# A graph network on one core: reordered transfers, masks kept from layer to layer, and products of exact bf16 parts

## The chip, the core and the metric

The kernel runs on one core of a Trainium2 chip. The metric is device time in microseconds, lower is better; the kernel before is a median of three runs. The engines are called here as the profile calls them: PE (TensorE, with PEld for its weight loads), DVE (VectorE), ACT (ScalarE), POOL (GpSimd) and SP (SyncE, which only issues transfers here). [...]

## What is computed

Two graph-attention layers and a two-layer perceptron, on 6,250 nodes of 768 features and 100,000 edges sorted by destination:

```python
h = jnp.maximum(_layernorm(x, axis=-1), 0.0)
# gat_conv, with 4 heads in layer 1 and 1 head in layer 2; every node also has an edge to itself
h = (x @ W).reshape(n, heads, -1)
alpha_s = (h * a_src[None]).sum(-1)
alpha_d = (h * a_dst[None]).sum(-1)
e = jax.nn.leaky_relu(alpha_s[src] + alpha_d[dst], NEG_SLOPE)
...
alpha = e / (denom[dst] + 1e-16)
out = jax.ops.segment_sum(h[src] * alpha[:, :, None], dst, num_segments=n)
# after both layers, each followed by relu
h = jax.nn.relu(h @ Wm1 + bm1)
return h @ Wm2 + bm2        # and x + this is the result
```

The hidden width is 256 and everything is float32.

## The kernel before

The nodes are cut into 49 tiles of 128 (the last has 106). The edges, padded, make 784 tiles of 128, in 196 groups of four; a group's destinations lie in a moving window of nodes that steps by 32.

**Stage 1** (the loop over `i` with `moments`, `spread_means`, `centre`, `features1`, `keep1`, from line 252) normalizes x and multiplies it by W1. For a tile, x comes twice, as rows (`xt`, for the statistics) and transposed (`xTt`, for the product), each 384 KB. DVE computes mean and variance; PE spreads the means over the free dimension by a product with the identity (L218); DVE subtracts (L224), ACT takes relu, PE makes six products of 128x264 (L233), and ACT and POOL put the row together that goes to `table1` in HBM (L244). The loop runs three tiles ahead with its moments and fetches five tiles ahead. W1 has eight more columns, W1 times the attention vectors, which PE computes from the transposed weights (`scores_in`, L147). The edge indices are loaded on ACT's queue, and `edge_places` turns them, piece by piece between the tiles, into places inside the window: `dcol` as columns, `dmod_d` as bf16 rows in HBM.

**Edge layers** (`layer_edges`, run for layer 1 and then for layer 2). POOL gathers the source rows of each edge tile from the table (L339), ten groups ahead, one indirect transfer for every tile. `fetch_rows` (L349) broadcasts 16 tiles of `dmod_d` to all partitions, and `make_mask` (L362) compares them with the partition number: a bf16 0/1 mask of eight tiles, that is, of two groups. PE multiplies the masks with the destinations' factors (L383). `pair` computes the weights of two tiles (ACT L401, L403, DVE L406 and following), and PE adds up the rows by destination in `o_ps` (L429). `gather_up` folds a group's sum into the running sum (L442); finished strips of 32 nodes are copied to `sum` (L455), and with the last strip of a node tile its steps are appended to `late`, to be run one at a time between the pairs by `advance`.

**Node work.** In layer 1, `Node1` adds the node's own edge, divides, transposes, multiplies by W2 and writes `table2` (L552). In layer 2, `Node2` does the same and then the perceptron; `prefetch` loads the node's row and x, `ahead` adds the bias bm2, broadcast to all partitions, to x (L617), and the last steps add that to the product in `y_ps` (L646, L650) and store the result (L651).

The order on each engine is the program's order inside the blocks under `tc.manual_schedule()`, of which there are three, one for each stage; between them a scheduler places what stands outside. [...]A tile of a pool comes free when its last reader is done.

Of the kernel before, what the change touches and what calls it, by code (L numbers as in the profile page):

```python
# [47 lines left out]
def kernel(  # L48
# [39 lines left out]
    make_identity(nc, ident)  # L88
    iota = const.tile([P, P], F32, name="iota")
# [53 lines left out]
    def scores_in(ps, w, wt, a, K, H):  # L143
        p = ps.tile([P, K, 2 * H], F32, name="aps", tag="e")
        for k in range(K):
            for j in range(KH):
                nc.tensor.matmul(p[:, k], wt[:, j, k * P:(k + 1) * P], a[:, j],  # L147
                                 start=(j == 0), stop=(j == KH - 1))
        nc.vector.tensor_copy(w[:, :, HID:], p)

    def load_x(xp, i):
        n = min(P, N - i * P)
        t = xp.tile([P, IN_DIM], F32, name="xt", tag="xt")
        if n < P:
            nc.vector.memset(t, 0.0)
        nc.sync.dma_start(t[:n], x[i * P:i * P + n])
        return t, n
# [4 lines left out]
    def edge_places(ones):  # L162

        dst_i = ones.tile([P, NET], I32, name="dst_i")
        nc.scalar.dma_start(dst_i, dst_cols)
        dri = ones.tile([NCH, CH], I32, name="dri")
        nc.scalar.dma_start(dri, dst_rows)
        nc.scalar.dma_start(src_i, src_cols)
        for layer in bT:
            with nc.allow_non_contiguous_dma(reason="256 numbers"):  # L170
                nc.scalar.dma_start(bT[layer], {1: b1, 2: b2}[layer].rearrange("(k p) -> p k", p=P))
        yield
# [15 lines left out]
        nc.scalar.dma_start(dmod_d, drm)  # L188
# [3 lines left out]
    bT = {layer: const.tile([P, KH], F32, name=f"bT{layer}") for layer in (1, 2)}  # L192
    with tc.tile_pool(name="w1p", bufs=1) as wp, tc.tile_pool(name="x1", bufs=6) as xp, \
            tc.tile_pool(name="wk1", bufs=3) as wk, tc.tile_pool(name="once", bufs=1) as ones, \
            tc.manual_schedule():
        xs, xTs, means, cents, rs = {}, {}, {}, {}, {}

        def fetch(i):
            xs[i], _ = load_x(xp, i)
            xTs[i] = xp.tile([P, KI, P], F32, name="xTt")  # L200
            nc.sync.dma_start(xTs[i], xT[i].rearrange("p (k n) -> p k n", k=KI))

        def moments(i):
# [9 lines left out]
            means[i] = mv, std, rstd  # L213

        def spread_means(i):
            mv, _, rstd = means[i]
            m_ps = ps.tile([P, P], F32, name="mean_ps", tag="n")
            nc.tensor.matmul(m_ps, mv[:, 0:1].to_broadcast([P, P]), ident, start=True, stop=True)  # L218
            means[i] = m_ps, rstd
# [26 lines left out]
        fetch(0)  # L246
        loaded = weights_in(wp, W1T, A1, KI, 4, "w1")
        fetch(1)
        w1 = wp.tile([P, KI, HID + 8], F32, name="w1")
        nc.sync.dma_start(w1[:, :, :HID], W1.rearrange("(k p) f -> p k f", p=P))  # L250
        for i in range(2, 5):
            fetch(i)
        pieces = edge_places(ones)
        next(pieces)
        for i in range(-3, NT):
            if i == 0:
                scores_in(ps, w1, *loaded, KI, 4)
            if 0 <= i:
                if i + 5 < NT:
                    fetch(i + 5)  # L260
                h = features1(i)
            if i + 3 < NT:
                moments(i + 3)
            if 0 <= i + 2 < NT:
                _, std, rstd = means[i + 2]
                nc.vector.reciprocal(rstd, std)
                spread_means(i + 2)
            if 0 <= i + 1 < NT:
                centre(i + 1)
            if 0 <= i:  # L270
                keep1(i, *h)
                if i >= 2:
                    next(pieces, None)
# [42 lines left out]

    def layer_edges(layer, H, node, pre, matched):
# [3 lines left out]
        with tc.tile_pool(name=f"g{layer}", bufs=AHEAD + 2) as gp, \  # L321
                tc.tile_pool(name=f"rows{layer}", bufs=3) as rows, \
                tc.tile_pool(name=f"eg{layer}", bufs=2) as eg, \
# [3 lines left out]
            G, drow, mask, hot, e_ps, o_ps = {}, {}, {}, {}, {}, {}  # L327
# [5 lines left out]
            def gather(g):  # L333
                if not 0 <= g < NG:
                    return
                G[g] = gp.tile([P, TPG, TW[layer]], F32, name="G")
# [5 lines left out]

            def fetch_rows(r):

                k = 16 * r
                if 0 <= k < NET:
                    drow[r] = rows.tile([P, 16 * P], BF16, name="drow")
                    n = min(16, NET - k) * P
                    nc.sync.dma_start(drow[r][:, :n], bcast(dmod_d, n, k * P))  # L349
# [5 lines left out]
            def make_mask(u):  # L355

                if not 0 <= u < NU:
                    return
                a, b = (t * P for t in both(u))
                mask[u] = eg.tile([P, 8 * P], BF16, name="mask")  # L360
                at = u % 2 * 8 * P
                nc.vector.tensor_scalar(mask[u][:, a:b], drow[u // 2][:, at + a:at + b], pidx, None,  # L362
                                        ALU.is_equal)

# [69 lines left out]
            def gather_up(g):  # L434
# [3 lines left out]
                acc = sums.tile([P, RW[layer]], F32, name="acc")  # L438
                if g == 0:
                    nc.vector.tensor_copy(acc, o_ps.pop(g))  # L440
                else:
                    nc.vector.scalar_tensor_tensor(acc, run[0], keep[:, (g + 1) % 4:(g + 1) % 4 + 1],  # L442
                                                   o_ps.pop(g), ALU.mult, ALU.add)
                run[0] = acc
                a = g - 2
                if a < 0:
                    return
                t, q = divmod(a, 4)
                if q == 0:
                    done[t] = sums.tile([P, RW[layer]], F32, name="sum", bufs=3)  # L450
                    node.prefetch(t)
                if q == 2:
                    node.ahead(t)
                r = slice(32 * q, 32 * q + 32)
                nc.scalar.activation(done[t][r], acc[r], AF.Copy)  # L455
                if g == NG - 1:
                    node.ahead(t)
                    nc.vector.tensor_copy(done[t][64:], acc[64:])
                    q = 3
                if q == 3:  # L460
                    late.append(node.steps(t, done.pop(t)))
# [7 lines left out]
            for r in range(3):  # L469
                fetch_rows(r)  # L470
            for u in range(2):
                make_mask(u)
# [6 lines left out]
            for g in range(NG):  # L479
# [7 lines left out]
                else:  # L487
                    if g % 4 == 0:
                        fetch_rows(g // 4 + 3)
# [6 lines left out]
                hot.pop(g, None)  # L496
            gather_up(NG - 1)
# [18 lines left out]
    with tc.tile_pool(name="w2p", bufs=1) as wp, tc.tile_pool(name="wk2", bufs=2) as wk:  # L516
        w2 = with_scores(ps, wp, W2, W2T, A2, KH, 1, "w2")

        class Node1:
# [12 lines left out]
            def steps(self, t, sum_):  # L532
# [13 lines left out]
                for k in range(KH):  # L546
                    nc.tensor.matmul(h_ps, rT[:, k], w2[:, k], start=(k == 0), stop=(k == KH - 1))
# [7 lines left out]
        with tc.tile_pool(name="pre1", bufs=1) as pre:  # L555
            pre1 = prepare(pre, 1, 4)
            with tc.manual_schedule():
                layer_edges(1, 4, Node1(), pre1, lambda: None)


    with tc.tile_pool(name="wmp", bufs=1) as wp, tc.tile_pool(name="x3", bufs=3) as xp, \
            tc.tile_pool(name="wk3", bufs=2) as wk, tc.tile_pool(name="pre2", bufs=1) as pre, \
            tc.manual_schedule():
# [3 lines left out]
        bm2b = wp.tile([P, OUT_DIM], F32, name="bm2b")  # L567
# [4 lines left out]
        def matched():  # L572
# [6 lines left out]
            nc.scalar.dma_start(bm2b, bcast(bm2, OUT_DIM))  # L579
# [20 lines left out]
        class Node2:  # L600
            rows, xs = {}, {}

            def prefetch(self, t):
# [4 lines left out]
                nc.sync.dma_start(self.xs[t][0][:n], x[t * P:t * P + n])  # L608
# [6 lines left out]
            def ahead(self, t):  # L615
                xt, n = self.xs[t]
                nc.vector.tensor_add(xt[:n], xt[:n], bm2b[:n])  # L617

            def steps(self, t, sum_):
# [23 lines left out]
                for s in range(2):  # L643
                    y_ps[s] = ps.tile([P, half], F32, name="y_ps", tag="n")
                    for j in range(KH):
                        nc.tensor.matmul(y_ps[s], mT[:, j], wm2[:, j, s * half:(s + 1) * half],  # L646
                                         start=(j == 0), stop=(j == KH - 1))
# [3 lines left out]
                nc.sync.dma_start(out[t * P:t * P + n], y[:n].rearrange("p s f -> p (s f)"))  # L651
# [301 lines left out]
```

## Time and profile before

| | |
|---|---|
| timed runs | 2784.78 us (2783.95 to 2788.01) |
| the profiled execution | 2218.71 us, span 2216.9 us |
| mean granted PE clock | 0.808 |
| gathers, L339 | 1564, 962 ns each |
| HBM read and written | 335.80 MB and 32.50 MB |

The profiled execution was a quarter shorter than the timed ones. All rows of the profile below belong to the shorter one.

The page cuts the span into 40 slices of 55 us. Stage 1 fills the first three and a part of the fourth, layer 1 goes from 187 to 1180 us, layer 2 from there to the end. In the tables a group of instructions has its busy time, the mean of one in ns, and then the idle time of its engine ahead of it with what ended most of it. "Issue" means that the engine waited for nothing that the profile shows. In the rows of the timeline the columns are start, duration, engine, line, operation, output and inputs with their shapes, count, and in brackets the idle time before and its releaser. In the rows of windows they are the window, its length, and for PE, PEld, DVE, ACT and POOL the busy time with the number of instructions, then PE's granted clock, the busy share of the DMA engines and GB/s.

### The profile page before, as it was taken

Reading aid. Unit: us, or ns where it says so; the run is one execution under the profiler, and the core shown is the slowest. Engines: PE = TensorE matmul, PEld = TensorE weight load, DVE = VectorE, ACT = ScalarE, POOL = GpSimd, SP = SyncE. Lnnn points to the kernel's source line nnn. Section 1 sums busy time; section 2 is a strip of 40 time slices with the busy share of each in tenths; the row PEclk is TensorE's granted clock in tenths of the full one; section 3 lists DMA queues with packets and bytes.
Section 4 is the critical chain, followed back from the end, with each engine's and each line's share of the span. In section 5 each row is a group of like instructions: output and inputs, shape, how many; then the busy total and the mean of one; then the engine's idle time right before and its main releaser. Section 6 shows DMA issues by size and latency. Waiting matters only on the chain. (4 is left out here: it accounts for less than half of the span.)

```text
span 2216.9 us, 25764 instructions
## 1 busy us (share of the span) xinstructions
PE 1581.7 (71%) x6588; PEld 1099.4 (50%) x6589; DVE 1480.5 (67%) x4510; ACT 599.4 (27%) x2602; POOL 1518.4 (68%) x1672
## 2 busy tenths in 40 slices
PE   7995766676667676666675777677877777777776
PEld 6783444444444444444443455555555554555553
DVE  6665677777777677777775666666666666666663
ACT  3552222222222222222222222222222222222221
POOL 0004777777777777777775777777777777777773
PEclk9997777877887877887886798888777878778786
DMA  8893555555555555545545565565556556555652
GB/s 288 291 306 109 143 145 151 151 139 148 152 152 141 146 151 151 150 139 150 151 122 172 162 182 158 183 182 165 177 181 182 166 174 183 171 166 182 181 143 89
DMA packets 149839, 370.16 MB, mean 167 GB/s; under 512 B 34354, under 2 KB 60978, under 8 KB 149684
## 3 DMA queue, kind: packets, MB, share of 16 engines
q0 software_dynamic: 75072, 209.10, 35.0%
q1 hardware_dynamic: 72052, 156.47, 21.3%
q10 hardware_dynamic: 2560, 2.86, 0.4%
q8 instruction: 56, 0.92, 0.2%
q14 instruction: 99, 0.81, 0.1%
HBM read 335.80 MB, written 32.50 MB: 166 GB/s over the span
## 5 line engine op out<-in xcount | busy, mean ns | idle before, releaser
L339 POOL DMA_INDIRECT G<-table,src_i x1564 | 1504.4, 962 | 496.1 <-issue 404.8
L429 PE MATMUL o_ps<-hw,hot 128*128 128x260 f32 x1564 | 590.8, 514 | 319.0 <-DVE hw L418 310.9
L429 PE MATMUL o_ps<-G,hw 128*128 128x258 f32 x1564 | 564.2, 497 | 260.2 <-DVE hw L413 255.9
L429 PEld LDWEIGHTS o_ps<-hw,hot 128*128 128x128 f32 x1564 | 345.1, 244 | 503.8 <-DVE hw L418 436.2
L429 PEld LDWEIGHTS o_ps<-G,hw 128*128 128x128 f32 x1564 | 339.2, 238 | 425.5 <-DVE hw L413 371.7
L406 DVE TENSOR_TENSOR e_ps<-e,e_ps 128x8 f32<-128x8 f32 (+1 forms) x782 | 129.6, 166 | 550.9 <-ACT e L403 550.8
L455 ACT ACTIVATE sum<-acc 32x260 f32<-32x260 f32 (+1 forms) x388 | 161.7, 417 | 696.7 <-DVE acc L442 695.5
L413 DVE TENSOR_SCALAR hw<-iota_ps,dcol,w 128x128 f32<-128x128 f32 x782 | 285.0, 406 | 14.4
L401 ACT ACTIVATE e<-G 128x8 f32<-128x8 f32 (+1 forms) x782 | 158.9, 203 | 471.1 <-DMA G<-table,src_i 452.1
L418 DVE TENSOR_TENSOR hw<-G,e_ps 128x520 f32<-128x520 f32 x391 | 271.8, 695 | 14.5 <-DVE e_ps L416 1.2
L442 DVE SCALAR_TENSOR_TENSOR acc<-acc,keep,o_ps 128x260 f32<-128x260 f32 (+1 forms) x390 | 185.7, 476 | 3.3 <-PE o_ps L429 3.3
L233 PE MATMUL h_ps<-w,r 128*128 128x264 f32 x588 | 146.5, 401 | 13.2 <-ACT r L226 13.1
L403 ACT ACTIVATE e<-G 128x8 f32<-128x8 f32 (+1 forms) x782 | 150.0, 192 | 0.2
L646 PE MATMUL y_ps<-wm,mT 128*128 128x384 f32 x392 | 143.1, 488 | 1.3 <-ACT mT L640 0.9
L372 DVE TENSOR_TENSOR hot<-iota_ps,dcol 128x512 f32<-128x512 f32 (+1 forms) x196 | 133.8, 682 | 0.0
L233 PEld LDWEIGHTS h_ps<-w,r 128*128 128x128 f32 x588 | 112.2, 197 | 33.5 <-ACT r L226 15.5
L243 POOL COPY row<-sd 128x4 f32<-128x4 f32 x49 | 9.1, 186 | 170.0 <-ACT sd L242 170.0
L512 ACT ACTIVATE rT<-tp,bT 128x128 f32<-128x128 f32 x196 | 61.2, 363 | 159.6 <-PE tp L505 159.3
L362 DVE TENSOR_SCALAR mask<-drow,pidx 128x1024 bf16<-128x1024 bf16 (+1 forms) x196 | 96.4, 493 | 2.2 <-DMA drow<-dmod_d 2.2
L383 PEld LDWEIGHTS <-mask 128*128 128x128 bf16 x1564 | 73.3, 101 | 42.6 <-issue 18.4
L646 PEld LDWEIGHTS y_ps<-wm,mT 128*128 128x128 f32 x392 | 74.2, 190 | 34.1 <-ACT mT L640 1.4
L207 DVE BATCH_NORM_STATS2 stats<-xt 128x6 f32<-128x384 f32 x98 | 49.9, 551 | 51.0 <-DMA xt<-in_x 50.4
(385 smaller groups left out, 1091.4 us busy)
## 6 DMA issues: line engine op xcount, KB each, us to landing
drow<-dmod_d SPq DMA_DIRECT2D x98, 512.0 KB, 5.6
xt<-in_x SPq DMA_DIRECT2D x96, 384.0 KB, 4.2
G<-table,src_i POOLq DMA_INDIRECT x1564, 2.8
xTt<-in_xT SPq DMA_DIRECT2D x49, 384.0 KB, 4.7
out<-y SPq DMA_DIRECT2D x48, 384.0 KB, 3.3
table<-row SPq DMA_DIRECT2D x49, 132.0 KB, 3.5
row<-table SPq DMA_DIRECT2D x49, 130.0 KB, 5.6
table<-row SPq DMA_DIRECT2D x49, 129.0 KB, 2.8
```

What stands on the lines that cost most here:

```text
L233: nc.tensor.matmul(h_ps, r[:, k], w1[:, k], start=(k == 0), stop=(k == KI - 1))
L339: nc.gpsimd.indirect_dma_start(out=G[g][:, t], out_offset=None, in_=table[layer], in_offset=bass.IndirectOffsetOnAxis(ap=src_i[:, k:k + 1] ...
L372: nc.vector.tensor_tensor(hot[g][:, T[0]:T[0] + n], iota_ps.unsqueeze(1).to_broadcast([P, n, P]), dcol[:, k:k + n].unsqueeze(2).to_broadca ...
L401: nc.scalar.activation(e1, sc, AF.Exp)
L403: nc.scalar.activation(e2, sc, AF.Exp, scale=SLOPE)
L406: nc.vector.tensor_mul(v, e2, rho)
L413: nc.vector.tensor_scalar(hw[:, t], iota_ps, dcol[:, k:k + 1], w[:, t], ALU.is_equal, ALU.mult)
L418: nc.vector.tensor_mul(hw, G[g][:, T, :RW[1]].rearrange("p t (h c) -> p t h c", h=H), w.unsqueeze(3).to_broadcast([P, 2, H, C + 1]))
L429: nc.tensor.matmul(o_ps[g], l, r[:, :RW[layer]], start=(k == tiles(g)[0]), stop=(k == TPG - 1))
L442: nc.vector.scalar_tensor_tensor(acc, run[0], keep[:, (g + 1) % 4:(g + 1) % 4 + 1], o_ps.pop(g), ALU.mult, ALU.add)
L455: nc.scalar.activation(done[t][r], acc[r], AF.Copy)
L646: nc.tensor.matmul(y_ps[s], mT[:, j], wm2[:, j, s * half:(s + 1) * half], start=(j == 0), stop=(j == KH - 1))
```

## The change

It has six parts:

- **Order of the first transfers.** Only tile 0's x goes ahead of W1's transposed weights; then come tile 0's transposed x, W1, and tile 1. The scores' product is done before tile 1 is looked at. The edge indices move from ACT's queue to SP's, between the tiles.
- **Loads and stores of 106 rows** are split in 96 and 10 rows (`runs`); the last store also in two column halves.
- **Means as bf16 products.** From tile 2 on, POOL splits the mean in three bf16 parts whose sum is exact (`in_parts`), and PE makes three bf16 products in place of one float32 product.
- **Layer 2's masks from layer 1.** Layer 1 stores each mask in HBM (`mask_d`, 256 KB for two groups), and layer 2 loads it instead of fetching the rows and comparing again.
- **The last bias on PE.** bm2 is split in three bf16 parts; a product of ones (3x128) with them (3x384) starts each accumulation of `y_ps`, and the addition to x in `ahead` is gone.
- **Smaller ones.** One manual schedule spans all stages; the pools of gathered rows, rows and masks are shared by both layers; the last group's sum is used where it lies; `prefetch` and `ahead` are called some groups earlier; W2's scores are computed inside layer 1's start.

```diff
+        eng.tensor_copy(parts[0], f)
+        eng.tensor_sub(a, f, parts[0])
+        eng.tensor_copy(parts[1], a)
+        eng.tensor_sub(b, a, parts[1])
+        eng.tensor_copy(parts[2], b)
...
+        return [(a, b) for a, b in ((0, n // 16 * 16), (n // 16 * 16, n)) if a < b]
...
-        nc.sync.dma_start(t[:n], x[i * P:i * P + n])
+        for a, b in runs(n):
+            nc.sync.dma_start(t[a:b], x[i * P + a:i * P + b])
...
-        nc.scalar.dma_start(dst_i, dst_cols)
-        nc.scalar.dma_start(dri, dst_rows)
-        nc.scalar.dma_start(src_i, src_cols)
+        for to, of in ((dst_i, dst_cols), (dri, dst_rows), (src_i, src_cols)):
+            nc.sync.dma_start(to, of)
+            yield
+            yield
...
-            nc.tensor.matmul(m_ps, mv[:, 0:1].to_broadcast([P, P]), ident, start=True, stop=True)
+                for k in range(3):
+                    nc.tensor.matmul(m_ps, parts[:, k:k + 1].to_broadcast([P, P]), ident_b,
+                                     start=(k == 0), stop=(k == 2))
...
-        fetch(0)
+        fetch_x(0)
         loaded = weights_in(wp, W1T, A1, KI, 4, "w1")
-        fetch(1)
+        fetch_xT(0)
         w1 = wp.tile([P, KI, HID + 8], F32, name="w1")
         nc.sync.dma_start(w1[:, :, :HID], W1.rearrange("(k p) f -> p k f", p=P))
-        for i in range(2, 5):
-            fetch(i)
+        for i in range(1, 5):
+            fetch_x(i)
+            fetch_xT(i)
         pieces = edge_places(ones)
-        next(pieces)
-        for i in range(-3, NT):
-            if i == 0:
-                scores_in(ps, w1, *loaded, KI, 4)
+        moments(0)
+        spread_means(0)
+        sc1 = scores(ps, *loaded, KI, 4)
+        centre(0)
+        nc.vector.tensor_copy(w1[:, :, HID:], sc1)
+        for i in range(-2, NT):
...
+                if layer == 2:
+                    return fetch_mask(u + 1)
...
                 nc.vector.tensor_scalar(mask[u][:, a:b], drow[u // 2][:, at + a:at + b], pidx, None,
                                         ALU.is_equal)
+                nc.sync.dma_start(mask_d[u * P:(u + 1) * P], mask[u])
...
+                if last:
+
+                    late.append(node.steps(t, acc))
...
                     if g % 4 == 0:
-                        fetch_rows(g // 4 + 3)
+                        if layer == 1:
+                            fetch_rows(g // 4 + 3)
+                        node.prefetch(g // 4)
+                    else:
+                        node.ahead(g // 4)
...
+                if layer == 1 and g == NG - 3:
+                    for k in range(3):
+                        fetch_mask(k)
...
-                nc.vector.tensor_add(xt[:n], xt[:n], bm2b[:n])
+                pass
...
+                    nc.tensor.matmul(y_ps[s], ones_r, bm2r[:, s * half:(s + 1) * half],
+                                     start=True, stop=False)
                     for j in range(KH):
                         nc.tensor.matmul(y_ps[s], mT[:, j], wm2[:, j, s * half:(s + 1) * half],
-                                         start=(j == 0), stop=(j == KH - 1))
+                                         start=False, stop=(j == KH - 1))
                     yield 1
                 for s in range(2):
                     nc.vector.tensor_add(y[:n, s], y_ps[s][:n], xt[:n, s * half:(s + 1) * half])
-                nc.sync.dma_start(out[t * P:t * P + n], y[:n].rearrange("p s f -> p (s f)"))
+                    if t == NT - 1:
+                        for a, b in runs(n):
+                            nc.sync.dma_start(out[t * P + a:t * P + b, s * half:(s + 1) * half],
+                                              y[a:b, s])
+                if t < NT - 1:
+                    nc.sync.dma_start(out[t * P:t * P + n], y[:n].rearrange("p s f -> p (s f)"))
```

## The prediction

> **What bounds the kernel now.** I read the page's busy totals and slices first, then windows over the two edge layers, then the gathers' starts in the timeline, and last the timeline at the four places where GpSimd is idle.
>
> ```profile
> PE 1581.7 (71%) x6588; PEld 1099.4 (50%) x6589; DVE 1480.5 (67%) x4510; ACT 599.4 (27%) x2602; POOL 1518.4 (68%) x1672
> ...
> PEclk9997777877887877887886798888777878778786
> DMA  8893555555555555545545565565556556555652
> ...
> L339 POOL DMA_INDIRECT G<-table,src_i x1564 | 1504.4, 962 | 496.1 <-issue 404.8
> 187.00:1170.00 983.00, 659.19 (x2626) 432.02 (x2625) 709.30 (x1998) 239.46 (x1162) 743.92 (x782) 0.79 0.53 145
> 1186.00:2185.00 999.00, 739.71 (x3168) 517.57 (x3168) 640.47 (x2186) 262.20 (x1204) 760.48 (x782) 0.80 0.58 173
> ```
>
> The totals name no bound: four engines are at 67 to 71%. The windows do. 782 gathers lie in each layer, and no other engine is above 74% busy there. GpSimd's gap before a gather is nearly always "issue": it waits for no one. In the timeline a gather starts 1.25 us after the last one (0.95 busy, 0.30 issue) almost without exception. So the layers last as long as their gathers: 187.83 to 1168.70 is 781 steps of 1.256 us, 1186.64 to 2184.07 is 781 of 1.277. Against 1.25 they lose 4.6 and 21.2 us. The time to win is in four places: before the first gather (188 us), between the layers (17 us), after the last gather (33 us), and those 21 us.
>
> ```profile
> 1507.63 0.95 DVE L617 TENSOR_TENSOR xt<-xt,bm2b 128x768 f32<-128x768 f32 x1
> 1508.31 1.10 POOL L339 DMA_INDIRECT G<-table,src_i  x1 [0.30 <-issue]
> 1509.56 0.48 DVE L362 TENSOR_SCALAR mask<-drow,pidx 128x1024 bf16<-128x1024 bf16 x1
> 1509.71 1.15 POOL L339 DMA_INDIRECT G<-table,src_i  x1 [0.30 <-issue]
> 1511.16 0.95 POOL L339 DMA_INDIRECT G<-table,src_i  x1 [0.30 <-issue]
> ```
>
> In layer 2 the slow gathers stand beside two VectorE operations, the bias addition (L617) and the mask (L362). Summed over the layer, gathers beside L617 lose 9.4 us, those beside L362 10.1 us.
>
> ```profile
> 13.86 5.24 PEld L147 LDWEIGHTS aps<-w1a,w1T 128*128 128x128 f32 x24
> 19.60 5.02 PE L233 MATMUL h_ps<-w,r 128*128 128x264 f32 x12 [0.40 <-ACT r L226]
> 169.61 1.02 DVE L207 BATCH_NORM_STATS2 stats<-xt 128x6 f32<-128x384 f32 x2 [6.99 <-DMA xt<-in_x]
> 172.74 5.25 PE L233 MATMUL h_ps<-w,r 128*128 128x264 f32 x12 [5.66 <-ACT r L226]
> 1168.70 0.94 POOL L339 DMA_INDIRECT G<-table,src_i  x1 [0.30 <-issue]
> 1186.64 0.94 POOL L339 DMA_INDIRECT G<-table,src_i  x1 [17.00 <-DMA drow<-dmod_d]
> 2184.07 0.95 POOL L339 DMA_INDIRECT G<-table,src_i  x1 [0.30 <-issue]
> 2205.49 0.56 DVE L650 TENSOR_TENSOR y<-y_ps,xt 106x384 f32<-106x384 f32 x1 [0.73 <-PE y_ps L646]
> ```
>
> The first features wait until 19.6 us behind the scores' matmuls, themselves queued behind tile 1's mean. The last tile's x (106 rows), issued at 159.3, is there at 169.6; a 128-row load lands in a median of 4.2 us. The last y is written at 2206.05 and the span ends at 2216.9: the 106-row store takes 10.8 us, a full one 3.3.
>
> [...] Four o_ps records take 1.14 or 2.10 us here.
>
> **Part by part**, in us of the profile.
>
> *Start.* Only tile 0's x now stands before the scores' transposed weights, and W1 comes third, before x of tile 1; 1.2 MB of indices leave the first 20 us. Scores' weights land near 6; [...] W1 (2.4 MB at the 290 GB/s of the page's first slices[...]) lands near 11. TensorE then takes tile 1's mean, which needs x of tile 1 (3.1 MB: 13.2, an estimate). Features start near 13.7 instead of 19.6: **-6**.
>
> *Node means.* Two fp32 records (0.36 of the tile's pitch, the rest being 2.53 of weight loads) become three bf16 products with their own weight loads. The mask products, 8 in 0.47 at most, give 0.06 each: 0.18. The tile pitch is 2.89 now, so 2.71; 47 tiles give -8.5 if TensorE limits. But 0.92 MB a tile in 2.71 us is 340 GB/s, and the best 20 us window moves 327 with the DMA engines 94% busy. I take 2.8 us, **-4**, with 0 and -8.5 as ends. The five GpSimd operations a tile (about 1 us, from 0.19 for its copy of a few columns) wait for the tile's moments; behind them on GpSimd stands only the table row of three tiles before, which nobody reads in this stage. GpSimd has 1.4 us of work in 20, and the products are used a tile later: hidden.
>
> *Stalls in stage 1.* 49 tiles at 2.89 should end near 163; they end at 183.6. Of the 20, about 8 belong to the last tile's x, now split in 96 and 10 rows; about 5 lie at 60 to 76 us, where the 1.5 MB of `drow` was fetched early and VectorE stood on it; that fetch now follows the last table row. The rest is x coming late and may stay. **-10**, ends -8 and -13. The start as a whole: **-20** (ends -14, -27).
>
> *Layer 1.* 98 mask writes of 256 KB: 25.7 MB. At 145 GB/s for a 0.53 share they add 94 us of DMA time to 983: the share goes to 0.63. A gather has 40 tiles of lead, so **0**. On SyncE each store waits for VectorE's mask, and behind it stand the next `drow`, the node rows and layer 2's table rows: each has a group (5 us) or more to spare, and the mask precedes them on VectorE anyway. The `w2` scores now run after two mask stores in SyncE's queue, so the first pairs start some 5 us later; VectorE (72%) and TensorE catch up within the 50 us of lead: **0**.
>
> *Between the layers.* The last table row was issued at 1180.77, between fetches of 512 KB, and the first gather came 5.9 us later; a row store lands in 2.8. The masks now come from an earlier fetch: -3. The last sum is used without copying: -0.8. **-4**.
>
> *Layer 2.* L617 is gone, 98 masks are gone: **-19** of the 21.2. Instead 98 bias products of 3x384 bf16 run on TensorE. The trace has none of this width: at least 0.06, at most the 0.36 of an fp32 record of 384 columns; I take 0.2, 20 us on an engine 74% busy, hidden. The earlier prefetch of x waits on SyncE for the buffer of three tiles before, two groups after its release: 0.
>
> *Tail.* The last store in halves of 96 and 10 rows lands in about 3.3 plus one issue (0.4) instead of 10.8: -6.5. The 106-row load no longer stands in the gathers' way (ScalarE stood 3.8 us for one at 2184): -2.4. Sum used directly -0.8, bias products +0.3. **-9.5**.
>
> The split of bm2 into parts in stage 1 (five small VectorE operations, two transfers of kilobytes) lies under that stage's DMA and TensorE time: 0.
>
> Sum: -20 -4 -19 -9.5 = **-52 us** of 2217.
>
> **From profile to time.** The profiled execution took 2218.7, the timed ones 2784.8, 568 more, and the trace cannot say where. If everything is slower alike, -52 becomes -65; if it is a constant, or 0.36 us on each gather, it stays -52. I take the middle, -57: **2728**.
>
> **Rivals.** (a) *DMA keeps stage 1 where it is.* VectorE's 50 us of waits for x speak for it, the share of 0.9 too. Then the start gives -10: -42, times 1.13: 2737; with half of layer 2's losses staying as well, 2750. (b) *In the timed runs TensorE is slow and bounds the layers.* A slow clock would explain part of the 568, but with all records at half rate a group of layer 1 takes 5.0 us (two times 2.10, masks 0.2, a quarter of 0.63 and 1.93 for the node), one of layer 2 6.1 (0.63, 2.07 and 4.3), a tile of stage 1 6.0: 196 groups of each, 49 tiles and 60 us of gaps make about 2540 only. Then masks and the bias addition give nothing, the bias products cost up to 35, means -20, start -6, middle -3, tail -9: -3, 2782. (c) *The mask traffic slows the gathers*, which would be so if the unprofiled gathers are limited by DMA. A median landing of 2.8 us speaks against it. At most 94 us less 52: +42, 2827, slower.
>
> **Chances.** Forecast 0.67, (a) 0.16, (b) 0.08, (c) 0.09. The forecast's own ends are -45 x 1.0 and -70 x 1.26: 2740 and 2697. The range, 2696 to 2780, leaves out (c), most of (b) and a little beyond the low end. Faster 0.83, same 0.07, slower 0.10.
>
> **What would show it.** First gather near 168; a 1.255 us step in layer 2 and no 1.15 us gathers beside masks; 13 us between the layers; 23 us after the last gather; DMA share in layer 1 near 0.63 with gathers still landing in 2.8. A longer step in layer 1, or "DMA" as the releaser of GpSimd, would make it wrong; so would time that does not follow the span.

## The result: 0.8% slower, and a profile with another bound

The changed kernel takes 2805.36 us (2802.69 to 2808.06) where the kernel before, run beside it, takes 2784.36 (2777.70 to 2788.01): a ratio of 1.0078, 95% interval 1.0057 to 1.0100. The forecast was 2728. This time the profiled execution, 2805.3 us, is as long as the timed ones, so its rows show what the times are made of; the profile of the kernel before (2218.7 us) was of an execution a quarter shorter, and that difference turns out to be the subject of this study. Which chip that first profile came from is not known.

The page of the kernel after, engine totals, the gathers and the relu of the transposed node tile:

```profile
PE 1711.7 (61%) x6733; PEld 1136.8 (41%) x6734; DVE 1400.4 (50%) x4368; ACT 570.5 (20%) x2598; POOL 1554.9 (55%) x1908
...
L402 POOL DMA_INDIRECT G<-table,src_i x1564 | 1493.8, 955 | 1071.5 <-issue 831.7
L576 ACT ACTIVATE rT<-tp,bT 128x128 f32<-128x128 f32 x196 | 61.3, 363 | 703.7 <-remote 660.8
```

A gather lasts as long as ever (955 ns against 962), but GpSimd (POOL) idles 1071.5 us ahead of gathers, not 496. No other engine has become busy in its place: all are at 61% or less. New is ScalarE's 661 us of waiting ahead of L576 for "remote", a releaser that the profile can't name; in the profile before, the same line (L512) had 159 us, put down to TensorE's transposes. Windows over the two layers say the same:

```profile
178.00:1483.00 1305.00, 683.37 (x2484) 437.76 (x2484) 670.43 (x1891) 208.83 (x1094) 747.53 (x780) 0.70 0.45 129
1549.00:2737.00 1188.00, 784.50 (x3109) 514.45 (x3109) 535.24 (x1943) 240.22 (x1149) 740.54 (x780) 0.79 0.48 144
```

A layer has its 782 gathers, and no engine is busy for more than 45 us longer than in the profile before (VectorE is busy 105 us less in layer 2, without its masks and additions), but it lasts 1190 to 1308 us instead of 981 to 997. The DMA share is 0.45, not the 0.63 that I expected with the mask traffic, so transfers are no limit. The timeline at one node tile of layer 1 shows what is:

```profile
738.30 0.63 PE L569 MATMUL tp<-ident,o 128*128 128x128 f32 x2
739.23 2.10 PE L489 MATMUL o_ps<-hw,hot 128*128 128x260 f32 x4 [0.29 <-issue]
...
741.28 0.95 POOL L402 DMA_INDIRECT G<-table,src_i  x1 [0.30 <-issue]
...
748.82 0.63 ACT L576 ACTIVATE rT<-tp,bT 128x128 f32<-128x128 f32 x2 [13.41 <-remote]
749.24 2.09 PE L611 MATMUL h_ps<-w,rT 128*128 128x258 f32 x4 [7.91 <-ACT rT L576]
...
749.97 0.17 DVE L466 TENSOR_TENSOR e_ps<-e,e_ps 128x8 f32<-128x8 f32 x1 [7.72 <-ACT e L463]
```

The two transposes end at 738.93 by the profile's model. ScalarE, which waits on TensorE's semaphore alone here, goes on at 748.82, ten microseconds later. The trace holds the update of TensorE's semaphore that releases it, at 748.80, so it is the result that is late and not ScalarE. Behind L576 in its queue stand the sums and exponentials of the next groups; so VectorE stands (L466, 7.72), and TensorE, whose L611 takes `rT`, stands too (7.91). Only GpSimd goes on, with gathers up to the one at 745.03; the next is at 753.89, 7.91 us of idle time that the profile calls "issue" (that the buffers ahead were full then is my reading). A node tile takes some 27 us here (1308 us for 49) instead of 20.

### The profile page after: what moved, and what is told of

Its sections match the earlier page's. It is cut to its first block, busy times and chain, and to the rows that moved or that the text cites. A ratio compares the mean times of both kernels' runs of the same rounds, so it can differ in the third digit from the quotient of the medians.

```text
span 2803.5 us, 26481 instructions
## 1 busy us (share of the span) xinstructions
PE 1711.7 (61%) x6733; PEld 1136.8 (41%) x6734; DVE 1400.4 (50%) x4368; ACT 570.5 (20%) x2598; POOL 1554.9 (55%) x1908
## 4 chain that ended last, share of the span: by engine, by line
another core or an unknown queue 28%; DVE 24%; issue 18%; PE 16%; ACT 9%; DMA 3%; POOL 1%; SPq 0%; ACTq 0%; DVEq 0%; POOLq 0%
PE o_ps L489 7%; DVE hw L478 6%; DVE hw L473 4%; PE y_ps L713 4%; ACT sum L515 3%; DVE e_ps L466 2%; DVE acc L504 2%; ACT e L461 2%; PE m_ps L700 2%; PE h_ps L282 2%; DVE e_ps L476 2%; DVE mask L421 1%; DMA G<-table,src_i 1%; DVE y L717 1%
## 5 line engine op out<-in xcount | busy, mean ns | idle before, releaser
L402 POOL DMA_INDIRECT G<-table,src_i x1564 | 1493.8, 955 | 1071.5 <-issue 831.7
L489 PE MATMUL o_ps<-hw,hot 128*128 128x260 f32 x1564 | 606.8, 525 | 314.4 <-DVE hw L478 181.0
L489 PE MATMUL o_ps<-G,hw 128*128 128x258 f32 x1564 | 546.3, 487 | 289.1 <-DVE hw L473 193.4
L489 PEld LDWEIGHTS o_ps<-hw,hot 128*128 128x128 f32 x1564 | 353.8, 250 | 503.6 <-DVE hw L478 243.4
L466 DVE TENSOR_TENSOR e_ps<-e,e_ps 128x8 f32<-128x8 f32 (+1 forms) x782 | 128.5, 164 | 832.2 <-ACT e L463 583.5
L489 PEld LDWEIGHTS o_ps<-G,hw 128*128 128x128 f32 x1564 | 346.2, 238 | 437.6 <-DVE hw L473 247.8
L611 PE MATMUL h_ps<-w,rT 128*128 128x258 f32 x196 | 94.6, 633 | 312.7 <-ACT rT L576 272.3
L713 PE MATMUL y_ps<-wm,mT 128*128 128x384 f32 x392 | 187.3, 609 | 39.4 <-ACT mT L705 32.9
L576 ACT ACTIVATE rT<-tp,bT 128x128 f32<-128x128 f32 x196 | 61.3, 363 | 703.7 <-remote 660.8
L611 PEld LDWEIGHTS h_ps<-w,rT 128*128 128x128 f32 x196 | 54.7, 305 | 344.9 <-ACT rT L576 292.4
L717 DVE TENSOR_TENSOR y<-y_ps,xt 128x384 f32<-128x384 f32 (+1 forms) x98 | 53.7, 555 | 157.4 <-PE y_ps L713 73.6
L700 PE MATMUL m_ps<-rT,wm 128*128 128x128 f32 x392 | 72.5, 343 | 89.1 <-ACT rT L576 78.8
```

The costliest lines, as they stand in the source:

```text
L402: nc.gpsimd.indirect_dma_start(out=G[g][:, t], out_offset=None, in_=table[layer], in_offset=bass.IndirectOffsetOnAxis(ap=src_i[:, k:k + 1] ...
L466: nc.vector.tensor_mul(v, e2, rho)
L489: nc.tensor.matmul(o_ps[g], l, r[:, :RW[layer]], start=(k == tiles(g)[0]), stop=(k == TPG - 1))
L611: nc.tensor.matmul(h_ps, rT[:, k], w2[0][:, k], start=(k == 0), stop=(k == KH - 1))
```

## The experiments

Where a chip is named, it is because the sets ran on different ones, and that matters. All times of one set are from one chip and have the kernel before beside them.

### The kernel before once more, and three parts undone (chip 4)

`e1_before`: no edit.

> The kernel before, unchanged, profiled once more; its first profile took 2219 us where the timed runs took 2785. Theory 1 (in the timed runs TensorE's results come late: it is held back for some microseconds at a time, in both kernels, and the groups of both layers wait for it): an execution near 2785 us shows a step of about 1.7 us from gather to gather in layer 1 and 1.5 us in layer 2 as after's profile does, GpSimd idle for free G buffers, ScalarE idle about 12 us before L512 in each node tile, and semaphore updates of TensorE microseconds after the modelled ends. Rival (the change itself slows an otherwise gather-bound kernel): the step stays 1.25 us, with a time near 2220, or the 568 us lie elsewhere, for instance in 0.36 us more on each gather without idle TensorE.

Measured: 2717.9 us in the profiled execution, like the timed ones of this chip (2724.68 us median of 11). Its page:

```profile
L339 POOL DMA_INDIRECT G<-table,src_i x1564 | 1511.4, 966 | 948.3 <-issue 750.7
...
L512 ACT ACTIVATE rT<-tp,bT 128x128 f32<-128x128 f32 x196 | 61.3, 363 | 425.1 <-remote 354.5
```

So the kernel before has the late results as well. The recorded updates of TensorE's semaphore say it directly: of 1107 in this trace, 357 come more than 1 us after the modelled end of the last product that makes one; in the first profile it is 3 of 1381. VectorE's and ScalarE's updates come with the ends of their own instructions in both (1 of 2466 and 2 of 1648 later than 1 us here). From first to last gather its layers take 1222.0 and 1169.5 us: 1.56 and 1.50 us a gather, not 1.25. **GpSimd does not bound either kernel in the runs that the forecast was about.** The premise of the prediction was true of the execution that had been profiled and not of those runs.

`e2_masks_twice`: layer 2 compares again, nothing is stored.

```diff
-                if layer == 2:
-                    return fetch_mask(u + 1)
-                nc.sync.dma_start(mask_d[u * P:(u + 1) * P], mask[u])
```

> The kernel after with layer 2's masks computed again from dmod_d, as in the kernel before: no store of masks, no fetch of them. After stands at 1.0078 of before. Theory 2 (the stores of masks, or the queue of SyncE behind them, or the missing VectorE work, cost the loss): near 0.99 to 1.00. Theory 1 with the loss elsewhere: 1.005 to 1.010, as after. If the masks save what I forecast: 1.012 or more.

`e3_bias_add`: bm2 is broadcast and added to x in `ahead`, at its new place.

```diff
             def ahead(self, t):
-                pass
+                xt, n = self.xs[t]
+                nc.vector.tensor_add(xt[:n], xt[:n], bm2b[:n])
...
-                    nc.tensor.matmul(y_ps[s], ones_r, bm2r[:, s * half:(s + 1) * half],
-                                     start=True, stop=False)
```

> The kernel after with the last bias added by VectorE to x ahead of the sum, as in the kernel before: the 98 bias products L710 are gone. Theory 3 (TensorE sets the pace in the timed runs, and the products, for which a held-back TensorE has 20 us or more, cost the loss): 0.995 to 1.002, and layer 2 some 20 us shorter. If the products are hidden: 1.006 to 1.010, or up to 1.014 if the addition delayed gathers by 9 us.

`e4_fp32_means`: all means as one fp32 product.

```diff
-            if i >= 2:
+            if False:
                 parts = wk.tile([P, 3], BF16, name="mparts")
```

> The kernel after with all node means as fp32 products, as in the kernel before. If the bf16 means are worth what I forecast (4 us): 1.009. If they do nothing: 1.0078. If they bring TensorE's hold-ups about by doing more with less time [...]: 1.000 or less.

| kernel | us | ratio to before (95%) | layer 1, us | layer 2, us |
|---|---|---|---|---|
| before | 2724.68 | | 1222.0 | 1169.5 |
| masks twice | 2775.22 | 1.020 (1.017 to 1.023) | 1256.6 | 1201.0 |
| bias added | 2746.63 | 1.0091 (1.0063 to 1.0120) | 1259.3 | 1160.7 |
| fp32 means | 2785.79 | 1.0248 (1.0217 to 1.0278) | 1267.5 | 1191.1 |

(Layers are from the first gather's start to the last one's, in the one profiled execution of each.) None of the three brings the kernel to before's time, so none of these parts alone is the loss; all three keep layer 1 some 35 to 45 us too long. The first lies in the case "1.012 or more", the second in "hidden", and the third, expected at 1.009 at most, misses by far; as the kernel after itself was not run on this chip, what masks and means are worth there stays open. What the three share with the kernel after in layer 1 is, among other things, the place of `prefetch` and `ahead` (theory A below; B and C are its rivals). In layer 2 the version without products was the only quick one, which made the products suspect.

### The place of `prefetch` and `ahead` (chip 11)

`e5_after`: no edit. `e6_old_places`, from the kernel after; `e7_before_new_places` is the same edit the other way, on the kernel before:

```diff
                         fetch_rows(g // 4 + 3)
-                        node.prefetch(g // 4)
-                    else:
-                        node.ahead(g // 4)
...
                 t, q = divmod(g - 2, 4)
+                if t >= 0 and q == 0:
+                    node.prefetch(t)
+                if t >= 0 and (q == 2 or last):
+                    node.ahead(t)
```

`e8_products_twice`:

```diff
                                      start=True, stop=False)
+                    nc.tensor.matmul(y_ps[s], zeros_r, bm2r[:, s * half:(s + 1) * half],
+                                     start=False, stop=False)
```

> The kernel after, unchanged, beside the others on one chip, as the base of this set. Its first comparison gave 1.0078; on the chip of the last set I expect it above the version without the bias products (1.009), so 1.015 to 1.02 there, with layer 1 about 1255 to 1310 us from first to last gather and layer 2 about 1190.

> The kernel after with the nodes' rows fetched and their own terms multiplied (prefetch and ahead) where the kernel before does it: in gather_up, two groups later. Layer 1 alone took 1222 us before and 1257 to 1267 in three variants of after on one chip, whatever was done with masks, bias and means. Theory A (the multiplication L593, now ahead of the mask in the even group just before the sum's own VectorE work, shifts that work against TensorE's late results, and this is the loss in layer 1): layer 1 some 35 us shorter than in after beside it, ratio lower by 0.013. Theory B (the shorter, denser first stage leaves TensorE more held back for all of layer 1): no difference from after. Theory C (deeper mask buffers or the w2 scores at the start of layer 1): no difference either.

> The kernel before with prefetch and ahead at the places of after, and nothing else changed. Theory A: layer 1 longer by some 35 us, ratio 1.010 to 1.015. Theories B and C: 1.000, within 0.003.

> The kernel after with a second product of 3x384 bf16 (all-zero weights, adding nothing) behind each of the 98 bias products. In the last set layer 2 took 1190 to 1201 us with the products and 1161 without. If a held-back TensorE is what sets the time, and each product costs what it occupies there (30 us / 98 = 0.3 us): layer 2 another 30 us longer, ratio 0.011 above after. If the first product costs by its place in the queue (it opens the accumulation early) and not by its work: less than 8 us more.

This chip behaved otherwise: the kernel before took a median of 2219.19 us, and between 2212.63 and 2225.53 in all 21 runs, as in its first profile.

| kernel | us | ratio to before (95%) |
|---|---|---|
| after | 2174.47 | 0.9805 (0.9774 to 0.9837) |
| after, old places | 2177.82 | 0.9821 (0.9789 to 0.9853) |
| before, new places | 2209.72 | 0.9961 (0.9950 to 0.9971) |
| after, products twice | 2178.85 | 0.9815 (0.9783 to 0.9848) |

So where TensorE's results come on time the change wins 2%, 44.7 us. The kernel after on this chip, first its page, then windows over the layers, then the timeline's gathers at the end of layer 1 and the start of layer 2:

```profile
L402 POOL DMA_INDIRECT G<-table,src_i x1564 | 1485.0, 949 | 491.5 <-issue 397.6
...
L576 ACT ACTIVATE rT<-tp,bT 128x128 f32<-128x128 f32 x196 | 61.1, 362 | 160.8 <-PE tp L569 160.2
```

```profile
178.00:1155.00 977.00, 672.31 (x2620) 443.92 (x2620) 704.91 (x1993) 235.97 (x1160) 739.98 (x779) 0.77 0.60 174
1172.00:2147.00 975.00, 733.15 (x3258) 497.59 (x3258) 559.44 (x2037) 255.09 (x1204) 737.67 (x780) 0.86 0.59 177
```

```profile
1156.06 0.95 POOL L402 DMA_INDIRECT G<-table,src_i  x1 [0.30 <-issue]
1169.98 0.94 POOL L402 DMA_INDIRECT G<-table,src_i  x1 [12.98 <-DVE win L355]
```

Here "issue" ends most of the gathers' waits, with 0.30 us each (397.6 for 1305), and L576's 160 us are named again: TensorE's transposes. The loss itself does not occur on this chip, so the same four were run again.

### The same four where results are late (chip 13)

> The kernel after once more, as the base. The last set ran on a chip on which the kernel before takes 2219 us in every run, as in its first profile, and after 2174: there TensorE's results come on time. On a chip where before takes about 2720 to 2785 I expect 1.008 to 1.02, layer 1 at 1255 to 1310 us; on one where it takes 2219, 0.980 again.

> After with prefetch and ahead at the places of the kernel before. On a chip where TensorE's results come late (before near 2750 us). Theory A (place of the multiplication): layer 1 some 35 us shorter than in after beside it, ratio lower by 0.013. Theories B (denser first stage) and C (mask buffers, w2 scores): as after, within 0.004. On a chip where they come on time: as after, 0.980 to 0.982, as in the last set.

> Before with prefetch and ahead at the places of after. Where TensorE is late. Theory A: layer 1 longer by 35 us, 1.010 to 1.015. Theories B and C: within 0.003 of 1. Where it is on time: 0.996, as in the last set.

> After with a second, all-zero product behind each bias product. Where TensorE is late and its work sets the time of layer 2: layer 2 longer by another 20 to 30 us, 0.007 to 0.011 above after. If the first product costs by its place: less than 8 us more. Where TensorE is on time both are hidden: 0.980 to 0.982, as in the last set.

| kernel | us | ratio to before, 2778.00 us (95%) | layer 1, us | layer 2, us |
|---|---|---|---|---|
| `f1_after` | 2801.31 | 1.0107 (1.0069 to 1.0145) | 1299.3 | 1185.9 |
| `f2_old_places` | 2766.30 | 0.9965 (0.9950 to 0.9979) | 1267.8 | 1188.2 |
| `f3_before_new_places` | 2821.23 | 1.0154 (1.0108 to 1.0201) | 1290.3 | 1198.9 |
| `f4_products_twice` | 2807.52 | 1.0107 (1.0064 to 1.0149) | 1304.0 | 1204.3 |

The layer 1 of the first two, by their first and last gathers in the timeline, `f1_after` and then `f2_old_places`:

```profile
176.49 1.32 POOL L402 DMA_INDIRECT G<-table,src_i  x1 [2.65 <-DMA table<-row]
...
1475.75 0.95 POOL L402 DMA_INDIRECT G<-table,src_i  x1 [0.30 <-issue]
```

```profile
176.64 1.32 POOL L402 DMA_INDIRECT G<-table,src_i  x1 [2.65 <-DMA table<-row]
...
1444.49 0.95 POOL L402 DMA_INDIRECT G<-table,src_i  x1 [0.30 <-issue]
```

On this chip theory A holds both ways. Putting two calls back takes 35 us off the kernel after (31 of them in layer 1 of the profiles) and makes it quicker than before; moving them forward alone costs the kernel before 43 us. The same edit, on the same kernel, gave 9.5 us on the chip where results are on time. Doubling the products costs nothing that can be told (1.0107 both times; the medians are 6 us apart); the 18 us more in layer 2 of its profile, an execution of 2825 us, lie inside the spread of its runs (2795.4 to 2827.0).

### Which of the two, and what if L576 stands later (chip 15)

`g1_add_old_places` is `e3_bias_add` with the old places. `g3_ahead_alone_old` moves back only `ahead`. `g2_relu_later` has the old places and

```diff
                 p = turn(o)
                 yield 1
+                yield 1
+                yield 1
                 rT = straighten(wk, 1, p)
```

in layer 1 (two steps later), and one more `yield 1` in layer 2. `g4_all_three` is `g2_relu_later` with the bias added by VectorE.

> After with two parts undone: the bias added by VectorE (no products), prefetch and ahead at the old places. On a chip where TensorE is late, old places alone gave 0.9965. If the products cost what layer 2 showed (25 to 30 us): 0.985 to 0.988. If they cost nothing: 0.996. On a chip where it is on time: 0.984 (the addition delays gathers by 9 us).

> After with prefetch and ahead at the old places, and the relu of the transposed node tile (L576) with all that follows it two half-groups later in layer 1 and one later in layer 2. Theory 1a (ScalarE, in order, stands about 8 us a node tile for the late transposes, and the sum copies and exponentials behind it starve VectorE and then TensorE: the loop that sets the pace): ScalarE finds the transposes done more often, its wait before L576 falls from some 400 us to under half, layer 1 shorter by 50 to 150 us, 0.94 to 0.98. Theory 1b (TensorE is simply that slow, and the wait only moves to the next operation that needs it): time unchanged, 0.990 to 1.003, with the waits at acc (L504) or row (L614) instead. Where TensorE is on time: 0.980 to 0.984.

> After with only the multiplication (ahead) at its old place, the row fetch (prefetch) at its new one. If the multiplication's place is what matters: as with both at the old places, 0.996. If the fetch's place: as after, 1.008 to 1.011. Where TensorE is on time: 0.980 to 0.982.

> The bias added by VectorE, old places and the later relu together: the candidate for the fastest where TensorE is late. If theory 1a and the products' cost both hold: 0.93 to 0.97. If only the products' cost holds: as the first of this set, 0.985 to 0.988. If neither: 0.996. Where TensorE is on time: 0.984 to 0.988, slower than after by the delayed gathers.

| kernel | us | ratio to before, 2722.55 us (95%) | layer 1, us | layer 2, us |
|---|---|---|---|---|
| `g1_add_old_places` | 2742.13 | 1.0060 (1.0036 to 1.0084) | 1228.6 | 1201.5 |
| `g2_relu_later` | 2699.77 | 0.9915 (0.9896 to 0.9934) | 1235.9 | 1155.2 |
| `g3_ahead_alone_old` | 2736.14 | 1.0040 (1.0014 to 1.0065) | 1228.6 | 1194.7 |
| `g4_all_three` | 2686.94 | 0.9863 (0.9843 to 0.9883) | 1227.3 | 1157.6 |

Layer 1 is equally short with `ahead` alone at its old place as with both (1228.6, in one profile of each), so what counts there seems to be the multiplication, L593: at its new place it stands with the mask in the group whose sum `Node1` is about to take up. But the whole time of the third run, 1.0040, is not the 0.996 that I expected, and its layer 2 was no better than after's; whether the fetch's place costs there, or the chips differ, was not tried. The first run, with both calls at their old places, misses too: 1.0060, where 0.996 was the highest expectation. So the move of the calls accounts for the loss on chip 13, and on chip 15 something else keeps these versions 14 and 20 us above before. The first run speaks against the products as the cause of the loss in layer 2: without them, with the addition at its old place, layer 2 took 1201.5 us. The quick layer 2 of `e3_bias_add` came from something else, perhaps the order; this stays open.

The later relu gives 0.9915, inside what theory 1b expected and far from 1a's 0.94 to 0.98. In layer 2 it gains some 40 us. In layer 1 it does not gain. Between 300 and 1400 us ScalarE's wait before the relu in `g1_add_old_places`, and then waits of `g2_relu_later`, are

```profile
ACT rT L577 <- remote: 408.9, 41, 13.8
```

```profile
ACT sum L519 <- issue: 330.4, 63, 11.4
...
DVE acc L504 <- remote: 205.8, 29, 13.2
...
ACT row L617 <- remote: 112.8, 33, 10.2
```

Of the 390 to 410 us of "remote" before ScalarE's relu in that stretch of the first and third kernels of the set, 24 are left, and VectorE at `acc` and ScalarE at `row`, which also take results of TensorE, stand in its place. The late result is paid for here by whoever asks next. ("Issue" is less sure here than in the first profile: updates are missing from the traces of long executions, in `after` all but 2491 of VectorE's 4286, and a wait without its update can look like none.) Still `g4_all_three`, 36 us below before, has the lowest ratio of all versions where results are late; its 0.9863 lies in the band of "only the products' cost holds", but the first run doesn't support that reading, so the agreement is luck; where they are on time it was not run.

### Less work for TensorE (chip 2)

`h1_before_narrow` and `h2_after_narrow`, from before and from after:

```diff
-                    nc.tensor.matmul(o_ps[g], l, r[:, :RW[layer]], start=(k == tiles(g)[0]),
+                    n = RW[layer] if k == tiles(g)[0] else 65
+                    nc.tensor.matmul(o_ps[g][:, :n], l, r[:, :n], start=(k == tiles(g)[0]),
```

> The kernel before, but of the four products of a group (o_ps, L429) only the first covers all 260 or 258 columns; the other three cover 65. It leaves out the rest of those sums; every instruction, weight load, transfer and wait stays. The matmul time of o_ps falls to 0.44. On a chip where before takes 2720 to 2785: if TensorE's work there makes its results late and these set the pace (theory 1), the gathers come back to near 1.25 us and the time to 2200 to 2350, 0.80 to 0.86. If results are late whatever TensorE does: 2650 or more, over 0.95. Where before takes 2219 (gathers set the pace): 2190 to 2219.

> The kernel after with the same columns of o_ps left out. If theory 1 holds: the gathers set the pace again and the change gives its 45 us, so 45 us below the narrowed kernel before (2155 to 2305 us). If the loss of after has nothing to do with TensorE's lateness: equal to or above the narrowed kernel before.

Measured: 2721.98 us beside 2725.25, a ratio of 0.9992 (0.9980 to 1.0004), and 2753.49 us, 1.0110 (1.0073 to 1.0147). Both miss what theory 1 gave for them, 0.80 to 0.86 and 45 us below the narrowed before: the columns of these products are not what makes its results late. The number of products, the weight loads and the node work are as before in these runs, so they are not cleared. The page's row of TensorE's granted clock and then layer 1's window, both of `h1_before_narrow`, and below them layer 1's window of `e1_before`:

```profile
PEclk9985555555555555555555556666666666666567
```

```profile
188.00:1415.00 1227.00, 602.86 (x2476) 469.42 (x2476) 667.00 (x1880) 209.32 (x1092) 749.24 (x779) 0.51 0.42 115
```

```profile
190.00:1410.00 1220.00, 701.31 (x2476) 444.24 (x2476) 665.64 (x1879) 209.57 (x1094) 751.21 (x780) 0.69 0.43 116
```

TensorE's matmuls are busy 14% less in layer 1, the granted clock falls from 0.69 to 0.51, and the layer is as long as before. A lower clock came with less work, and together they left the pace where it was. And the change costs as much with TensorE relieved (1.1%) as without.

## Why the prediction was wrong

**The bound** was read rightly from its profile and was not that of the timed runs. (Three engines, not four, are at 67 to 71% there; the bound was read from the windows and does not rest on it.) In the profile of before, a gather follows a gather after 1.25 us; in `e1_before`, after 1.50 to 1.56.

**The parts** can be checked on chip 11, where the bound is the one that the prediction assumed, profile against profile:

| stretch | before | after | measured | forecast |
|---|---|---|---|---|
| to the first gather | 187.8 | 174.8 | -13.0 | -20 |
| layer 1 | 980.9 | 981.2 | +0.3 | 0 |
| between the layers | 17.9 | 13.9 | -4.0 | -4 |
| layer 2 | 997.4 | 977.7 | -19.7 | -19 |
| after the last gather | 32.8 | 24.0 | -8.8 | -9.5 |
| sum | | | -45.2 | -52 |

The timed difference there is -44.7. Four of the five terms are right to 1 us. (A bias product has 0.33 us of record in that trace, where 0.2 was taken, and stays hidden all the same.) In the first one, the step that failed is *node means*: with three bf16 products the tiles of stage 1 still follow each other in 2.89 us (features at 151.18, 154.07 and 156.97), not in 2.80; that term is 0, not -4. TensorE's first features start at 14.45, 5.2 us earlier (forecast 6), and the rest, -8, is what is left of the stalls' -10. That 106 rows in pieces of 96 and 10 would land about as fast as a full tile was an estimate of mine. In `after` the last x is used 5.4 us after its issue (155.13 to 160.52), where before took 10.3; the last store takes 6.1 us (y written at 2797.39, span end 2803.5), where before took 10.8 and I had 3.7.

**From profile to time** is the step that decided the sign. I took the 568 us between profile and timing for something that scales or adds, and made -57 of -52 (the middle of the two cases named is -58.5, a slip of no weight). It was another bound: each node tile waits for late results of TensorE, and what the change takes from GpSimd and the transfers inside the layers only lengthens GpSimd's idle time. Of the 45 us, `f2_old_places` keeps 11.7 (2778.00 to 2766.30); its first gather comes at 176.6, against 190.0 in `f3_before_new_places` on the same chip, which has before's first stage: 13.4 us, about as much. Between the layers 63.9 us pass in `e1_before` and in `f1_after` alike. So I take it that little but the start is left (argued, not isolated).

**A part costed at nothing.** Of the earlier `prefetch` I asked only whether SyncE would wait, and of the multiplication that moves with `ahead` in layer 1 not even that. On chip 13, where results are late, this move costs 35 us (`f1_after` less `f2_old_places`), and -11.7 + 35.0 = +23.3 is the loss on that chip. On chip 15 it is not the whole of it (`g1_add_old_places`, `g3_ahead_alone_old`).

**The rivals.** (b) put the timed runs down to TensorE and was right that its results bound the layers, but took the low clock for the cause and priced all records as where half the clock is granted (four of `o_ps` take a median of 2.09 us there and 1.14 at the full clock, in the first profile of before), which gave 2540 us; in the last set the clock fell further, to 0.596, and the time stayed. A second product cost nothing that can be told; the means were charged to it as a gain of 20 us, and `e4_fp32_means` without the kernel after beside it cannot say. (c), the only slower case, needed DMA to limit; the share was 0.45. The prediction's own warning, that "time that does not follow the span" would make it wrong, is what came true.

**What stays open** is why TensorE's results come late in most sets (the first comparison, and chips 2, 4, 13 and 15) and not on chip 11. It isn't the number of columns of its edge products. Nor is the clock settled: of the 208 updates of TensorE in the trace of `after` that come over 3 us late, 170 fall where half the clock is granted, 47% of the span; but half the clock over 33% of the span in the trace of chip 11, and over 38% in the first profile of before, went with 2 such updates each. Whether the low clock is a cause or follows from the waiting was not shown. One sign goes with lateness in these four traces: for the same 26,481 instructions of the kernel after, the trace of chip 11 holds 44,408 semaphore updates, that of `after` 16,605; for the kernel before, 41,818 in the short profile and 16,747 in `e1_before`. Where results are late, records are missing. That both have one cause is not shown by any run here, and engine by engine they don't go together: in `after` VectorE's updates are missing most (2491 of 4286 are there, of TensorE's 1214 of 1422), and yet 2 of VectorE's come over 1 us late and 372 of TensorE's. All runs of the sets have a recorded span and clock, so what the kernels take without recording is not known. Why an order of VectorE's work moves a layer by 30 to 40 us under late results is shown, but not explained.

## What to carry to other kernels

Before costing a change from a profile, compare the profiled execution's time with the timed runs: if they differ by a quarter, the profile may show another bound, and a factor between them is no model. An edit that only moves work off or around an engine that isn't the bound can change sign with the state of the chip: the same move of two calls gave 9.5 us on one and cost 43 on another, so measure both. When moving an instruction in an engine's queue, cost its new neighbours even where its own time is the same: here the move of `prefetch` and `ahead` cost 35 us on chip 13.

## What the runs showed of the hardware

- The kernel before took 2212.63 to 2225.53 us in its 21 runs on chip 11, and 2723 to 2784 (medians) in all sets on other chips. A short and a long profile of it differ by at most 5% in every engine's busy time (`before` and `e1_before`: TensorE's matmuls 1581.7 and 1657.6 us, VectorE 1480.5 and 1471.5, ScalarE 599.4 and 572.6, GpSimd 1518.4 and 1525.5).
- In the first profile of before, four products of `o_ps` took a median of 1.14 us where the full clock was granted and 2.09 us where half of it was.
- With three of four products in `o_ps` cut to 65 columns, TensorE's granted clock fell (0.768 in `e1_before`, 0.596 in `h1_before_narrow`, over the span) and the time stayed (2721.98 us beside 2725.25).
- In the slower executions only TensorE's semaphore updates were late: over 1 us behind the last modelled end in 372 of 1214 (`after`), in VectorE's 2 of 2491, in ScalarE's 2 of 1692. In the short profile of before it was 3 of 1381 of TensorE's, on the quick chip 2 of 1419 (`e5_after`).
- A result of two 128x128 transposes reached ScalarE ten microseconds after their modelled end (738.93 and 748.82 in `after`), while GpSimd's next five gathers went on in steps of 1.25 us.
- Stored in pieces of 96 and 10 rows, the last 106 rows took 6.1 us from the last y to the end of the span (`after`); in one piece they took 10.8 (`before`).
